# Two graph layers over one adjacency matrix: the first load of adj ahead of x, x in five parts, constants in another order

## The chip, the core and the metric

The kernel runs on one core of a Trainium2 chip. The metric is the device time of one execution in microseconds. The kernel before takes 233.75 us, the median of 3 runs (233.69 to 233.84).

## The reference

`x` has 4096 rows of 64 numbers, `adj` is 4096 x 4096 with zeros and ones (about one entry in 256 is a one), both in float32. Two layers follow one another; each adds its result to its input and normalizes every row (layernorm, no scale).

```python
# layer 0
support = x @ weight
rank = cumsum(adj != 0, axis=1); deg = rank[:, -1:]
k = minimum(deg, 100);  pos = rank - (deg - k)
w = mask * where(pos > 0, 0.5 ** (k - pos), 0)   # the last neighbour has weight 1,
x = layernorm(x + w @ support + bias)            # the one before it 1/2, then 1/4, ...
# layer 1
deg = max(sum(adj, axis=1) + 1, 1)
h = (adj @ x + x) / deg
o = relu(concat([x, h]) @ W + b);  o = o / max(norm(o), 1e-12)
x = layernorm(x + o)
```

In layer 0 the weight of a neighbour depends on how many neighbours with a higher column number the row has. So a row's sums are made from the highest column down, with a running count of the ones seen.

## The kernel before

**Tiling.** The host hands in adj transposed and cut into 8 slabs `g` of 512 rows (the output rows, along the free dimension) by 8 blocks `k` of 512 columns (the neighbours, on partitions, as 4 groups of 128). One such block is a tile `a` of 128 x 4 x 512. `load_next` (L102 to L109) fetches the next one with a DMA issued from GpSimd (POOL) that turns float32 into bfloat16: 512 KB in the core's memory, twice that in DRAM. There are 64 loads, in the order of the list `steps`: slab 0 from block 7 down to 0, then slab 1, and so on. 33 buffers hold them, three of which serve other tiles at first; 30 loads can therefore be resident. At most 8 loads are under way at a time: each load reuses the completion flag of the one eight before, so load 8 is issued when load 0 has landed. Adj stays resident because layer 1 reads each tile again.

**x.** `x` comes in two forms. `x_quads` (rows in the order in which the adj tiles hold their columns) goes to `xp`, which shares its memory with `c1`; `split_x` (L218) cuts a block of it into two float16 parts (`xhl`), with a cast, a subtraction on POOL and, in `split_x_low`, a scaling on VectorE. `x` in natural order goes to `x1` slab by slab with `load_x` (L126), and `add_b0` (L308) adds the bias of layer 0 to it. These loads and that of the weights (`load_weights`, L211) are issued from SyncE (SP), in one queue. Each DMA of `load_x` and `load_weights` first waits for a small memset of its target, which a compute engine carries out at the place in its own order where the function is called; that memset sets the time of the load.

**One step** (`g`, `k`). `count` (L317) counts the ones of a tile in 32 groups by 4 matmuls into one bank; VectorE adds the counts so far (`cs`). `spread` (L336) multiplies with `further`, a 128 x 128 matrix of zeros and ones, so that each group knows how many ones lie beyond it; ScalarE makes `near` of it. `weigh` (L343) runs 16 matmuls with `tri` (the ones within the same group) and 16 with `mine` (the group's own row of `near`) and then turns the exponent into a weight as 16-bit integers, read as bfloat16: ScalarE does two of the four groups (L367), VectorE the other two (L368). `gather` (L373) multiplies the weights of the step before with `xhl` into `acc0`. `some_sums` (L408) adds up to four matmuls of layer 1 for tiles whose `x1hl` is ready, so that the matrix engine has work while the others evict.

**Order.** Every engine's order is written out by hand. The loop over `chunks` (L711 on) runs one step after another; a chunk has one block in slabs 0 to 2, so there the count of the next step stands in each step, and up to four blocks later, so that several counts stand together. `load_next` is called once per step, ahead of the step's POOL work. `at(i, engine, fn)` hangs work into step `i` on an engine; `PLACES` overrides some of those places. Of the work named in the change: `split_x(k)` stands in steps 0 to 7 (block 7 first), `load_weights` at the end of step 1 on VectorE, `load_x(g)` in step 8g+3 and `add_b0(g)` in step 8g+7 on POOL, `prepare` (scales the weight of layer 0) in step 5, `bias_columns` in step 7, `centered_parts` (makes `wc_parts`) in step 9, `prepare_wx`, `products_parts` in step 10, `add_self(0)` in step 12, all on POOL. `early_px` (transposes with `ident16`) begins in step 3, `centered` (reads `cen`) stands in step 6, and `early_pu` (tiles `eu`, reads `wc_parts`) begins in step 9, on the matrix engine.

**Ahead of the loop.** POOL issues load 0, makes three index tables with iota (`dist`, `of_p`, `of_m`), and issues load 1 between them and loads 2 to 7 after them. SP issues x_quads in two halves of 512 KB. VectorE makes the constants one after another: `idle`, `pick`, `ident`, `cen`, `has`, `past`, `mine`, `tri`, two casts of `ident`, then `further` from the matmul `pf`. The matrix engine runs 14 matmuls on a tile of zeros, `pf`, the count of block 7, and then `warm(4)`, the spread, `warm(2)`; within step 0 `warm(4)` and `warm(3)` follow. The result of these warm-up matmuls is not used.

Of the kernel before, what the change touches and what calls it, by code (L numbers as in the profile page):

```python
# [10 lines left out]
BF16 = mybir.dt.bfloat16  # L11
# [4 lines left out]
ALU = mybir.AluOpType  # L16
# [3 lines left out]
DVE = mybir.EngineType.DVE  # L20
POOL = mybir.EngineType.Pool
SP = mybir.EngineType.SP

P = 128
R = 512
TB = R // P
KB = 4
Q = P // 4
MAX_NEIGH = 100
STEP = 128.0  # L30
# [7 lines left out]
HALVED = range(2, 7)  # L38
PLACES = {"centered_parts": (9, POOL), "prepare": (5, POOL), "bias_columns": (7, POOL), "prepare_wx": (10, POOL), "half_c1_b1 3": (38, POOL), "half_c1_b1 4": (46, POOL), "half_c1_b1 5": (57, POOL), "half_c1_b1 6": (62, POOL), "products_parts": (10, POOL), "first_mv 0": (10, "DVE, early"), "first_r 0": (11, "DVE, early"), "first_least 0": (13, "DVE, early"), "first_s 0": (11, ACT), "first_pu 0": (16, PE), "times_degree 0": (18, POOL), "first_least 1": (20, DVE), "first_pu 1": (24, PE), "first_mv 2": (28, DVE), "first_s 2": (29, ACT), "first_r 2": (29, DVE), "half_scale 2": (29, DVE), "first_x1 2": (30, POOL), "first_hi 2": (31, ACT), "first_xl 2": (31, POOL), "first_lo 2": (32, ACT), "first_least 2": (31, DVE), "half_high 2": (26, ACT), "half_rest 2": (26, DVE), "half_degree_out 2": (26, DVE), "half_degree 2": (26, PE), "half_low 2": (27, ACT), "half_pz 2": (27, PE), "half_y 2": (27, DVE), "first_x1 3": (37, POOL), "first_hi 3": (38, "ACT, late"), "first_least 3": (38, "DVE, early"), "half_low 3": (34, ACT), "half_b1 3": (38, POOL), "half_c1 3": (37, POOL), "first_s 4": (44, ACT), "half_scale 4": (45, "DVE, early"), "first_xl 4": (46, POOL), "first_least 4": (45, DVE), "first_lo 4": (47, "ACT, late"), "half_low 4": (42, ACT), "half_b1 4": (46, POOL), "first_s 5": (52, ACT), "half_scale 5": (53, DVE), "first_hi 5": (54, "ACT, late"), "first_least 5": (57, DVE), "half_low 5": (50, ACT), "half_b1 5": (52, POOL), "half_c1 5": (55, POOL), "first_s 6": (60, ACT), "first_xl 6": (62, POOL), "first_lo 6": (62, "ACT, late"), "half_low 6": (58, ACT)}
LAG = 1  # L40
SAVED = (15, 17, 18, 21, 27)


@with_exitstack
def adj_resnorm_kernel(
# [23 lines left out]
    nc = tc.nc  # L69
    D = x.shape[2]  # L70
    NG, NK = adjT.shape[0], adjT.shape[1]
# [4 lines left out]
    const = ctx.enter_context(tc.tile_pool(name="const", bufs=1))  # L76
# [25 lines left out]
    def load_next(n=1):  # L102
        for _ in range(n):
            s = next(loads, None)
            if s is None:
                return
            g, k = s
            a = a16p.tile([P, KB, R], BF16, tag="a16", name=f"a16_{g}_{k}")
            nc.gpsimd.dma_start(out=a, in_=adjT[g, k])  # L109
            A[g][k] = a  # L110
# [6 lines left out]
    xp = c1  # L117
# [1 line left out]
    prep = a16p.tile([P, KB * R // 2], F32, tag="a16", name="prep")  # L119
    xTs = [a16p.tile([P, KB, R], FP16, tag="a16", name=f"xT_{j}") for j in range(2)]  # L120

    def load_xp(k0, k1):
        bs = slice(k0 * KB, k1 * KB)
        nc.sync.dma_start(out=xp[:, bs, :], in_=x_quads[:, bs, :])

    def load_x(g):  # L126
# [1 line left out]
        nc.sync.dma_start(out=x1[:, ts(g, TB), :], in_=x[:, ts(g, TB), :])  # L128


    load_xp(NK // 2, NK)
    load_next()
    load_xp(0, NK // 2)
    dist = epi.tile([P, P], I32, tag="hT", name="dist")
    nc.gpsimd.iota(dist, [[1, P]], base=0, channel_multiplier=-1)
    load_next()
# [2 lines left out]
    nc.gpsimd.iota(of_p, [[4, KB], [4 * KB, NK], [1, 4]], base=0, channel_multiplier=-1)  # L139
    of_m = epi.tile([P, P], I32, tag="z", name="of_m")  # L140
    nc.gpsimd.iota(of_m, [[1, 4], [4 * KB, NK], [4, KB]], base=0, channel_multiplier=-1)
    load_next(6)

    idle = epi.tile([P, R], BF16, tag="near", name="idle")
    nc.vector.memset(idle, 0.0)
# [2 lines left out]
    quarters = [slice(e * Q, (e + 1) * Q) for e in range(4)]  # L148
# [10 lines left out]
    ident = epi.tile([P, P], F32, tag="near", name="ident")  # L159
    nc.vector.tensor_scalar(ident, dist, 0.0, None, ALU.is_equal)  # L160
    cen, wcf, b0T = prep[0:D, 0:D], prep[0:D, D : 2 * D], prep[0:D, 2 * D : 4 * D]
    w32, wc32 = prep[:, 4 * D : 6 * D], prep[:, 6 * D : 7 * D]
    nc.vector.tensor_scalar(cen, ident[0:D, 0:D], -1.0 / D, None, ALU.add)


    has = epi.tile([P, P], BF16, tag="y", name="has")
    nc.vector.tensor_scalar(has, of_p, 0.0, None, ALU.is_equal)
    past = epi.tile([P, P], BF16, tag="hT", name="past")
# [9 lines left out]
        else:  # L178
            nc.vector.tensor_scalar(mine[quarters[e]], one_hot, STEP, None, ALU.mult)

    tri = const.tile([P, Q], BF16, name="tri")
    for rows in quarters:
        nc.vector.tensor_scalar(tri[rows], dist[rows, rows], 0.0, -STEP, ALU.is_lt, ALU.mult)
        nc.vector.scalar_tensor_tensor(
            tri[rows], ident[rows, rows], STEP * MAX_NEIGH, tri[rows], ALU.mult, ALU.add
        )
    most = const.tile([P, 1], F32, name="most")
    nc.vector.memset(most, MAX_NEIGH)
    less = const.tile([P, 1], F32, name="less")
# [14 lines left out]
    nc.vector.memset(power, -0.5)  # L204
    x1T = const.tile([P, R], FP16, name="x1T")
    ident16 = const.tile([P, P], FP16, name="ident16")
    nc.vector.tensor_copy(ident16, ident)
    ident_b = const.tile([P, P], BF16, name="ident_b")
    nc.vector.tensor_copy(ident_b, ident)

    def load_weights():  # L211

# [104 lines left out]
    def count(g, k, first, last):  # L317
        if first:
            cnt[g] = ps_m.tile([P, R], F32, tag="m", name=f"cnt_{g}_{k}")
        for q in range(KB):  # L320
            nc.tensor.matmul(  # L321
                cnt[g][quarters[q], :],
                lhsT=pick[:, PW - 4 * k : PW - 4 * k + Q],
                rhs=A[g][k][:, q, :],
                start=first,
                stop=last,
            )
        if last:
            new = one.tile([P, R], BF16, tag="cs", name=f"cs_{g}_{k}")
            if g in cs:  # L330
                nc.vector.tensor_tensor(new, cnt[g], cs[g], ALU.add)  # L331
            else:
                nc.vector.tensor_copy(new, cnt[g])  # L333
            cs[g] = new

    def spread(g, k):  # L336

        pr = ps_m.tile([P, R], F32, tag="m", name=f"rep_{g}_{k}")
        nc.tensor.matmul(pr, lhsT=further, rhs=cs[g], start=True, stop=True)  # L339
        near[g] = epi.tile([P, R], BF16, tag="near", name=f"near_{g}_{k}")  # L340
        nc.scalar.activation(near[g], pr, AF.Relu, bias=most, scale=-1.0)  # L341
# [54 lines left out]
    def ready(i, g, b):  # L396
        k = b // KB
        return i >= low_at[k] + LAG and i >= when[g, k]

# [208 lines left out]
    def at(i, engine, fn, *args):  # L608
        i, engine = PLACES.get(" ".join([fn.__name__, *map(str, args)]), (i, engine))
        hooks[i, engine].append((fn, args))  # L610

    def run(i, engine):
        for fn, args in hooks.pop((i, engine), []):
            fn(*args)
# [5 lines left out]
    for k in range(NK):  # L620
        i = when[0, k]
        at(i, POOL, split_x, k)
        at(i, DVE, split_x_low, k)
    at(1, DVE, load_weights)
    at(NK - 2, POOL, prepare)
    at(NK + 1, POOL, prepare_wx)
    at(NK + 2, POOL, prepare_wn)
    for g in range(NG):
        at(NK * g + 3, POOL, load_x, g)
        at(NK * g + 7, POOL, add_b0, g)  # L630
        at(min(NK * g + 12, NS - 2), POOL, add_self, g)
    if HALVED:
        all_at(
# [12 lines left out]
    for g in range(NG - 1):  # L646
        i = NK * (g + 1)
# [42 lines left out]


    pi = ps_a.tile([P, R], F32, tag="acc1", name="pi")
    for i in range(14):
        nc.tensor.matmul(pi, lhsT=idle[:, 0:P], rhs=idle, start=True, stop=True)

    def warm(n):

        a = A[0][NK - 1][:, 0, :]
        for i in range(n):
            nc.tensor.matmul(pi, lhsT=a[:, 0:P], rhs=a, start=True, stop=True)  # L700
# [3 lines left out]
    further = const.tile([P, P], BF16, name="further")  # L704
    nc.vector.tensor_copy(further, pf)
    count(0, NK - 1, True, True)
    warm(4)
    spread(0, NK - 1)
    warm(2)
    held = None  # L710
    for c, chunk in enumerate(chunks):  # L711
        ahead = chunks[c + 1] if c + 1 < len(chunks) else []

        shares = [[]] * (len(chunk) - 1) + [ahead]
        nr = near[chunk[0][0]]
        for (g, k), share in zip(chunk, shares):
            i = when[g, k]
            run(i, ACT)
            load_next()
            run(i, POOL)  # L720

            w = weigh(g, k, nr) if i == 0 else None
            for s in share:
                count(*s, s == ahead[0], s == ahead[-1])
            run(i, "DVE, early")
            w = w or weigh(g, k, nr)
            run(i, "ACT, late")
            if i == 0:
                warm(4)
            n_todo = len(todo)  # L730
            done = some_sums(i, 0 if i in SAVED else QUOTA)
            half = 0
            if share and share[-1] == ahead[-1]:
                if held is not None and len(todo) == n_todo:

                    half = KB // 2
                    gather(*held, 0, half)
                spread(*ahead[-1])
            if i == 0:
                warm(3)  # L740
            if done is not None:
                evict_part(done)
            if held is not None:
                gather(*held, half)
            held = (g, k, w)
            if g > 0 and k == NK - 1:
                first_hT(g - 1)
            run(i, PE)
            run(i, DVE)
# [318 lines left out]
```

## Time and profile before

| | us |
|---|---|
| median of 3 runs | 233.75 |
| the profiled execution | 233.72 |
| its span, first to last instruction | 231.7 |
| PE busy (matmuls) | 209.5 |
| DVE busy (VectorE) | 182.2 |
| ACT busy (ScalarE) | 140.6 |
| POOL busy (GpSimd) | 112.3 |
| adj loads: 64 x 512 KB, median from issue to landing | 15.2 |
| x_quads: 2 x 512 KB, the same | 4.5 |
| x in natural order: 8 x 128 KB | 7.2 |
| weights: 192.5 KB | 7.2 |

The durations in the prediction come from the profiled execution, which is 0.03 us below the median. The page cuts the span into 40 slices of 5.8 us and gives each engine's busy share in tenths. A group names the line, the engine, the operation, output<-inputs, shapes and count, then the busy time and the mean of one in ns, then the idle time of the engine just before these instructions with what ended most of it. In a stretch's line the numbers are: its length, busy time (and number of instructions) of PE, PEld (weight loads of the matrix engine), DVE, ACT and POOL, the granted clock of the matrix engine, the busy share of the 16 DMA engines, and GB/s. The share may come out a little over 1. In the lines on queues, q0 carries the loads issued from POOL, q1 those from SP; the numbers are packets, MB, and the time of the packets as a share of 16 engines. The bytes are those written.

### The profile page before, as it was taken

The page shows a single profiled execution, that of the slowest core. Times are in us where ns is not written, and L with a number is a line of the kernel's source. Part 1 is how long each engine was busy: PE and PEld are TensorE (multiplying, and loading weights), DVE is VectorE, ACT ScalarE, POOL GpSimd, SP SyncE. Part 2 cuts the span into 40 slices and gives each one's busy share as a digit, 9 for nine tenths or more (in the row PEclk, how much of TensorE's full clock was granted, in tenths as well). Part 3 has the DMA queues.
Part 4 walks back from the last instruction along what each step waited for, and adds up shares of the span by engine and source line. Part 5 has one row for each costly group of instructions (what it writes and reads, how often), then busy time and mean ns, then how long its engine had stood idle before and what let it go on. Part 6 is the DMA issues. An engine that isn't in the chain of part 4 may idle for free.

```text
span 231.7 us, 7494 instructions
## 1 busy us (share of the span) xinstructions
PE 209.5 (90%) x3138; PEld 95.2 (41%) x3178; DVE 182.2 (79%) x454; ACT 140.6 (61%) x212; POOL 112.3 (48%) x211
## 2 busy tenths in 40 slices
PE   7589999998998999999999999999999999999910
PEld 2133445443533443334333433443334344776810
DVE  6459877997797789798975996687678866599983
ACT  6057886687778767686557455664675451142684
POOL 7439677761537081641584056325433040079970
PEclk9799999999999999999999999999999999999975
DMA  6999999999999999999999999999970000000013
GB/s 201 209 213 219 215 216 213 217 217 214 215 219 212 214 214 223 211 214 214 218 217 207 200 183 210 204 195 181 205 168 4 3 0 0 3 0 1 23 45 113
DMA packets 11984, 37.36 MB, mean 161 GB/s; under 512 B 1328, under 2 KB 3504, under 8 KB 11952
## 3 DMA queue, kind: packets, MB, share of 16 engines
q0 software_dynamic: 9216, 33.56, 73.7%
q1 hardware_dynamic: 2736, 3.34, 4.7%
q8 instruction: 24, 0.39, 0.6%
q14 instruction: 8, 0.07, 0.1%
HBM read 69.40 MB, written 1.05 MB: 304 GB/s over the span
## 4 chain that ended last, share of the span: by engine, by line
PE 40%; DVE 11%; POOL 4%; ACT 3%; issue 2%; ACTq 0%; DVEq 0%; POOLq 0%
PE acc L378 12%; PE acc_part L387 11%; PE v L351 5%; PE cnt L321 3%; PE v L360 3%; ACT u L961 2%; POOL scratch L947 2%; DVE w L368 2%; POOL scratch L978 2%; DVE cs L331 1%; PE rep L339 1%; PE va L930 1%; PE pz L505 1%; PE vb L387 1%; DVE part L403 1%
## 5 line engine op out<-in xcount | busy, mean ns | idle before, releaser
L367 ACT ACTIVATE w<-v,less 128x1024 int16<-128x1024 f32 x64 | 71.3, 1113 | 43.7 <-PE v L360 31.7
L368 DVE TENSOR_SCALAR w<-v 128x1024 int16<-128x1024 f32 x64 | 78.2, 1221 | 13.0 <-PE v L360 12.1
L378 PE MATMUL acc<-w,xhl 128*128 128x512 bf16 x235 | 65.2, 380 | 1.9 <-issue 1.1
L109 POOL DMA_DIRECT2D a<-in_adjT_dram x64 | 36.9, 622 | 48.2 <-PE acc_part L387 25.4
L387 PE MATMUL acc_part<-a,x1hl 128*128 128x512 bf16 x140 | 38.2, 381 | 1.8 <-issue 1.3
L378 PEld LDWEIGHTS <-xhl 128*128 128x128 f16 x256 | 23.1, 98 | 33.6 <-issue 9.7
L341 ACT ACTIVATE near<-rep,most 128x512 bf16<-128x512 f32 x40 | 27.3, 682 | 8.7 <-PE rep L339 8.6
L387 PEld LDWEIGHTS <-x1hl 128*128 128x128 f16 x224 | 18.6, 98 | 31.1 <-issue 13.3
L351 PE MATMUL v<-a,tri 32*32 32x512 bf16 x1024 | 29.6, 384 | 0.3 <-DVE w L368 0.2
L360 PE MATMUL v<-near,mine 32*32 32x512 bf16 x1024 | 28.1, 376 | 0.0
L331 DVE TENSOR_TENSOR cs<-cnt,cs 128x512 bf16<-128x512 f32 x32 | 21.9, 686 | 4.4 <-PE cnt L321 4.0
L321 PE MATMUL cnt<-a,pick 128*32 128x512 bf16 x256 | 21.4, 389 | 4.2 <-DMA a<-in_adjT_dram 2.9
L351 PEld LDWEIGHTS <-tri 32*32 32x32 bf16 x1024 | 9.5, 87 | 21.7 <-issue 21.5
L339 PE MATMUL rep<-cs,further 128*128 128x512 bf16 x40 | 15.4, 385 | 1.5 <-DVE cs L331 1.1
L565 POOL TENSOR_SCALAR x<-y,mv_l,r_l 128x64 f32<-128x64 f32 x16 | 9.1, 575 | 12.4 <-DVE dr L516 6.4
L947 POOL TENSOR_TENSOR scratch<-scratch,power 128x4 f32<-128x4 f32 (+1 forms) x5 | 6.4, 1279 | 15.2 <-DVE scratch L949 15.1
L306 POOL TENSOR_TENSOR a<-a,ident_b 128x128 bf16<-128x128 bf16 x32 | 12.7, 431 | 0.1
L321 PEld LDWEIGHTS <-pick 128*32 128x32 bf16 x256 | 5.9, 94 | 14.8 <-issue 11.3
L333 DVE CAST cs<-cnt 128x512 bf16<-128x512 f32 x8 | 5.5, 692 | 7.8 <-PE cnt L321 7.8
L360 PEld LDWEIGHTS <-mine 32*32 32x32 bf16 x1024 | 10.2, 87 | 2.8 <-issue 2.4
L961 ACT ACTIVATE u<-u,scratch 128x64 f32<-128x64 f32 x27 | 9.8, 428 | 2.2 <-POOL scratch L980 2.1
L944 ACT ACTIVATE u<-u 128x256 f32<-128x256 f32 (+1 forms) x5 | 2.5, 502 | 12.1 <-DVE u L933 12.1
(177 smaller groups left out, 272.2 us busy)
## 6 DMA issues: line engine op xcount, KB each, us to landing
a<-in_adjT_dram POOLq DMA_DIRECT2D x64, 512.0 KB, 15.2
c<-in_x_quads_dram SPq DMA_DIRECT2D x2, 512.0 KB, 4.5
x<-in_x_dram SPq DMA_DIRECT2D x8, 128.0 KB, 7.2
out_dram<-u SPq DMA_DIRECT2D x8, 128.0 KB, 1.7
wts<-in_weights_dram SPq DMA_DIRECT2D x1, 192.5 KB, 7.2
```

Source lines behind the costliest of these rows:

```text
L109: nc.gpsimd.dma_start(out=a, in_=adjT[g, k])
L321: nc.tensor.matmul(cnt[g][quarters[q], :], lhsT=pick[:, PW - 4 * k : PW - 4 * k + Q], rhs=A[g][k][:, q, :], start=first, stop=last,)
L331: nc.vector.tensor_tensor(new, cnt[g], cs[g], ALU.add)
L339: nc.tensor.matmul(pr, lhsT=further, rhs=cs[g], start=True, stop=True)
L341: nc.scalar.activation(near[g], pr, AF.Relu, bias=most, scale=-1.0)
L351: nc.tensor.matmul(v[e // 2][quarters[q], e % 2, :], lhsT=tri[quarters[e], :], rhs=A[g][k][quarters[e], q, :], start=True, stop=False,)
L360: nc.tensor.matmul(v[e // 2][quarters[q], e % 2, :], lhsT=mine[quarters[e], 4 * k + q, :], rhs=nr[quarters[e], :], start=False, stop=True,)
L367: nc.scalar.activation(w[:, 0:2, :], v[0], AF.Relu, bias=less)
L368: nc.vector.tensor_scalar(w[:, 2:4, :], v[1], -STEP * MAX_NEIGH, 0.0, ALU.add, ALU.max)
L378: nc.tensor.matmul(acc0[g], lhsT=xhl[:, b, :], rhs=w[:, q, :].bitcast(BF16), start=(k, q) == (NK - 1, 0), stop=(k, q) == (0, KB - 1),)
L387: nc.tensor.matmul(acc, lhsT=x1hl[:, b, :], rhs=A[g][b // KB][:, b % KB, :], start=first, stop=last)
L961: nc.scalar.activation(o[:, t, :], y[:, t, :], AF.Identity, bias=off[:, t : t + 1], scale=r[:, t : t + 1])
```

## The change

- The first load of adj stands ahead of x in the program. The first SP load is the piece of x_quads for block 7 alone (128 KB). The other pieces (block 6; blocks 5 and 4; 3 and 2; 1 and 0) each wait for a memset on POOL: three of these stand between loads 2 to 7, the last in step 1.
- On VectorE `tri` is made right after `ident`, ahead of `has` and `past`; `cen` and the two casts of `ident` move behind the count of block 7, just ahead of the loop.
- The idle matmuls become 8 (were 14), and the later warm-up groups 1, 2, 3 and 3 (were 4, 2, 4 and 3).
- The weights are asked for in step 2 (was 1), the natural x of slab 0 in step 5 (was 3), and its bias is added in step 8 (was 7).

The parts of the program that compute are otherwise as before.

```diff
+WARM = 8, 1, 2, 3, 3
...
-    def load_xp(k0, k1):
+    def load_xp(k0, k1, held=True):
         bs = slice(k0 * KB, k1 * KB)
+        if held:
+            nc.gpsimd.memset(xp[:, k0 * KB, 0:1], 0.0)
         nc.sync.dma_start(out=xp[:, bs, :], in_=x_quads[:, bs, :])
...
-    load_xp(NK // 2, NK)
     load_next()
-    load_xp(0, NK // 2)
+    load_xp(NK - 1, NK, False)
     dist = epi.tile([P, P], I32, tag="hT", name="dist")
...
-    load_next(6)
+    load_next(2)
+    load_xp(NK - 2, NK - 1)
+    load_next(2)
+    load_xp(NK - 4, NK - 2)
+    load_next(2)
+    load_xp(NK - 6, NK - 4)
...
-    nc.vector.tensor_scalar(cen, ident[0:D, 0:D], -1.0 / D, None, ALU.add)
-
-
+
+    tri = const.tile([P, Q], BF16, name="tri")
+    for rows in quarters:
+        nc.vector.tensor_scalar(tri[rows], dist[rows, rows], 0.0, -STEP, ALU.is_lt, ALU.mult)
+        nc.vector.scalar_tensor_tensor(
+            tri[rows], ident[rows, rows], STEP * MAX_NEIGH, tri[rows], ALU.mult, ALU.add
+        )
     has = epi.tile([P, P], BF16, tag="y", name="has")
...
-    tri = const.tile([P, Q], BF16, name="tri")
-    for rows in quarters:
...
-    nc.vector.tensor_copy(ident16, ident)
...
-    nc.vector.tensor_copy(ident_b, ident)
...
-    at(1, DVE, load_weights)
+    at(1, POOL, load_xp, 0, NK - 6)
+    at(2, DVE, load_weights)
...
-        at(NK * g + 3, POOL, load_x, g)
-        at(NK * g + 7, POOL, add_b0, g)
+        at(NK * g + 3 if g else 5, POOL, load_x, g)
+        at(NK * g + 7 if g else 8, POOL, add_b0, g)
...
-    for i in range(14):
+    for i in range(WARM[0]):
...
-    warm(4)
+    warm(WARM[1])
     spread(0, NK - 1)
-    warm(2)
+    warm(WARM[2])
+    nc.vector.tensor_scalar(cen, ident[0:D, 0:D], -1.0 / D, None, ALU.add)
+    nc.vector.tensor_copy(ident16, ident)
+    nc.vector.tensor_copy(ident_b, ident)
     held = None
...
             if i == 0:
-                warm(4)
+                warm(WARM[3])
...
             if i == 0:
-                warm(3)
+                warm(WARM[4])
```

More of the change, by code (lines that the diff above doesn't have):

```diff
@@ L179, in adj_resnorm_kernel @@
             nc.vector.tensor_scalar(mine[quarters[e]], one_hot, STEP, None, ALU.mult)
-    tri = const.tile([P, Q], BF16, name="tri")
-    for rows in quarters:
[L183 to L186, printed above, removed]
     most = const.tile([P, 1], F32, name="most")
```

## The prediction

> **What bounds the kernel now.** I read the page first: its slices for where the time lies, its groups for who waits.
>
> ```profile
> PE   7589999998998999999999999999999999999910
> DMA  6999999999999999999999999999970000000013
> L321 PE MATMUL cnt<-a,pick 128*32 128x512 bf16 x256 | 21.4, 389 | 4.2 <-DMA a<-in_adjT_dram 2.9
> a<-in_adjT_dram POOLq DMA_DIRECT2D x64, 512.0 KB, 15.2
> ```
>
> Two rows are nearly full at once, the matmuls and the DMA engines, so it has to be settled which of them paces which stretch. Second view, stretches of time (length, busy time of PE, PEld, DVE, ACT, POOL, clock, DMA share, GB/s):
>
> ```profile
> 0.00:2.50 2.50, 1.32 (x4) 0.49 (x5) 0.71 (x10) 1.49 (x2) 1.35 (x7) 1.00 0.22 64
> 12.00:20.00 8.00, 6.98 (x125) 2.57 (x126) 5.38 (x9) 5.24 (x8) 4.53 (x8) 1.00 1.07 215
> 36.00:60.00 24.00, 22.69 (x429) 10.84 (x432) 20.30 (x41) 17.29 (x26) 14.14 (x31) 1.00 1.06 216
> 90.00:112.00 22.00, 21.12 (x356) 8.16 (x360) 19.57 (x43) 15.09 (x20) 7.68 (x14) 1.00 1.06 213
> 112.00:120.00 8.00, 7.80 (x125) 2.86 (x140) 6.40 (x14) 4.31 (x7) 6.66 (x13) 1.00 1.07 220
> 172.00:190.00 18.00, 17.79 (x275) 7.41 (x278) 15.83 (x37) 9.65 (x14) 4.80 (x9) 1.00 0.03 8
> ```
>
> The DMA share is above 1 from 2.5 us to beyond 120: one unbroken stream, in which a load of adj (0.524 MB) lands every 2.45 us. Third view, the order of time around the first count of each new load (start, length, engine, line, [idle before and what ended it]), and how long the loads issued at 9.2 and at 109.8 take to land:
>
> ```profile
> 8.94 0.62 PE L321 MATMUL cnt<-a,pick 128*32 128x512 bf16 x4 [2.67 <-DMA a<-in_adjT_dram]
> 27.87 0.10 PEld L321 LDWEIGHTS <-pick 128*32 128x32 bf16 x4 [0.45 <-DMA a<-in_adjT_dram]
> 30.62 0.23 PEld L321 LDWEIGHTS <-pick 128*32 128x32 bf16 x4 [0.17 <-DMA a<-in_adjT_dram]
> 118.80 1.05 PE L321 MATMUL cnt<-a,pick 128*32 128x512 bf16 x16
> ```
> ```profile
> L109 POOL DMA_DIRECT2D a<-in_adjT_dram x1: 535/535/535, 9.2 to 9.2; - x1
> ...
> DMA to landing us min/median/max: 21.4/21.4/21.4
> ...
> L109 POOL DMA_DIRECT2D a<-in_adjT_dram x1: 530/530/530, 109.8 to 109.8; - x1
> ...
> DMA to landing us min/median/max: 9.6/9.6/9.6
> ```
>
> TensorE waits 2.67 us for the first load (it lands at 1.23 + 7.7 = 8.9). It then catches up with the stream and waits for loads 7 and 8 (counted from 0; load 8 lands at 9.2 + 21.4 = 30.6, its count starts at 30.75). Load 10 lands at 17.2 + 18.4 = 35.6 and its count starts at 35.88. From there TensorE is slower than the stream and falls some us behind (the load issued at 53.46 lands 19.8 later at 73.2 and is counted at 77.3), until at 118.80 it wants loads 40 to 43 in a row: load 43 lands at 109.8 + 9.6 = 119.4, in the middle of those 1.05 us. So the stream touches the work at 28 to 36 us and again at 119; only a change that brings the stream forward brings the end forward.
>
> **The change part by part.** The 8 early adj loads and x share the 16 DMA engines, so I keep a ledger of the stream, in us of all 16 engines.
>
> Before, where adj starts: queue q0 (adj) had moved this much in the first 6 us and in the next 6, q1 (SP) beside it:
>
> ```profile
> q1 hardware_dynamic: 287, 1.05, 55.8%
> q0 software_dynamic: 35, 0.14, 13.0%
> ...
> q0 software_dynamic: 343, 1.27, 106.7%
> ```
>
> 1.41 MB by 12.0 us is 6.6 us at 214 GB/s: adj runs as if it had started at 5.4 at full rate. The 1.05 MB of x took 55.8% of 6 us, 3.35 us, before it.
>
> After, start S: one 128 KB piece of x goes first (first packets 1.7 us, about 0.5 us long) and adj load 0 is issued at 1.23 as before. What an adj load takes to its first packet on empty engines no row shows. Lower end: SP's x, issued at 0.73, has first packets at 1.7, so 1.0 us, S = 2.2. Upper end: as now, with no adj packet before 4.8, S = 4.9. Between: on busy engines the weights, issued at 18.57, have no packet before 21.4, about 2 us more than the 1.0 on empty ones, so I take the 2 off 4.9: S = 2.9.
>
> The Trainium skill ("DMA: Bandwidth & Descriptors", Latency and other measured facts) gives about 1 us to the first byte on this path; by it S would be 2.2 and the sum below -0.5 us. The row of 18.57 is weighed higher, as it is this kernel's.
>
> Cost X of the other 0.92 MB of x, now inside the stream: at the best pace of x alone (0.59 MB in 1.5 us, 404 GB/s) 2.3 us; at the price of the later x loads (128 KB in 1 KB packets; four of them 2.0% of 96 us, so 0.48 each) seven times 0.48, 3.4 us. One piece is such a 1 KB one, three have 2 KB packets, priced in between at 0.75: X = 0.48 + 2.25 = 2.7.
>
> Shift of the stream: (2.9 - 5.4) + 2.7 = +0.2 us. Ends: (2.2 - 5.4) + 2.3 = -0.9 and (4.9 - 5.4) + 3.4 = +2.9, the last only if x leaves the engines empty for 2.5 us.
>
> A rule that speaks against the change is in the same page (Rules for kernel authors): many small transfers should be one large one, at 2.0 us fixed per DMA. Three more DMAs would by it be +6 us and 239.9. The x rows above show 0.48 us of engine time for a whole one beside adj, so that figure is not used.
>
> What is gained on the way and lost again: load 0 lands at 2.9 + 2.45 + 1.1 = 6.5, 2.4 us earlier. The warm-up after the first count goes from 4 matmuls to 1; four of them ran 9.49 to 11.17 while the spread's input was ready at 10.29, so 0.9 us more. Step 1 starts some 3 us earlier. Steps 1 to 6 take 2.3 us each (counts at 16.0, 18.1, 20.4, 22.9, 25.2), so TensorE would be at count 6 by 22.5, and load 6 lands at about 25.2. All of the lead is waited away there.
>
> Work in cover of that lead: 8 instead of 14 idle matmuls (0.43 each): TensorE only waits for load 0 afterwards. The clock reads 0.67 and 0.65 in 7.5 to 12.5 now; a second stretch at half speed would double about 1.7 us of matmuls in step 1, and the 3 us pay for it. Constants: cen (1.25) and the two casts (0.23, 0.22) leave the way of `further` (ends 7.81, then about 6.5, load 0's own time) for DVE's 2.85 us of idleness before 13.14; without that cover they would cost 1.7. Four memsets of 0.1 on POOL and the later issue of loads 2 to 7: two loads, 5 us of transfer, are ahead of each. Where x comes late: the piece for step 1 is issued near 5 and by the later x rows (7.2 to landing) is there at 12, ScalarE's cast of it due at 16.08 - 3 = 13; behind that cast stand the evictions of step 1. The next pieces follow on SP's queue about 3.3 us apart (weights and x of slab 0, issued at 18.6 and 20.8, landed at 25.7 and 29.4) and are up to 1 us late for steps 2 and 4; the lead pays.
>
> SP's queue is now four pieces, weights, x of slab 0. The weights are asked for one step later in steps that come 2 to 3 us sooner: landing unchanged at 25.7, POOL's wait for them (1.64) too. x of slab 0 is two steps later, behind that wait: 25.7 + 0.95 (two multiplies) + 0.1, so issue near 26.8 instead of 20.8, landing 7.1 to 8.6 later at 33.9 to 35.4. Its 0.48 us leaves the stream ahead of load 8 and is back by load 10. add_b0, in step 8 now, waits for it on POOL (it had no wait at 30.21), and behind it stand load 17 (33.33 now; 7 loads still under way), centered_parts (1.53) and all to 40.2. 34.8 to 36.3 + 0.57 + 1.53 = 36.9 to 38.4 for wc_parts, which TensorE reads at 38.21: free, barely. POOL's backlog ends in its 1.48 us of idleness before 44.48.
>
> Sum: stream +0.2 us at loads 10 to 43, less nothing to speak of (0.06) at 119. Profiled execution: 233.72 (span 231.7 and 2.0 around it), the median 233.75. 233.75 + 0.2 = 233.95, said as 234.0. A shift under 0.2% (0.47 us) is about what a measurement of this kernel can tell from none.
>
> **The rivals.**
> - The stream gets longer (slower). For: adj's first packets may need more than 1.7 us, small packets are dear. Against: the first half of x was itself slow to start. It decides from S = 3.2 at X = 2.7; middle S = 3.6, X = 3.0: +1.2, 234.9.
> - x of slab 0 holds POOL, and wc_parts holds TensorE at 38.2 (slower). It decides when x lands after 35.2; if the weights land 1.5 us later than now, 1.7 us are lost, 235.4. For: the one queue in order. Against: the pieces ahead should be through by 21.4.
> - The stream gets shorter (faster): S = 2.2 to 2.5 and X = 2.3 to 2.5, -0.4 to -0.9, 232.85 to 233.35. For: the idle engines in 0 to 1.7 us and the 1.0 us of SP. Against: x takes 2.3 us wherever it stands.
> - All of the 2.4 us at load 0 stays (231.4). Against: the two waits at 27.87 and 30.62 and the tie at 119.4.
>
> **How the numbers follow.** No change to speak of 40% (233.3 to 234.2); longer stream 27% and POOL held 11%, slower together 38%; shorter stream 20% and full gain 2%, faster 22%. Leaving out 10% at either end, the range is 232.9 to 235.2: the low end is the -0.9, the high end +1.4, between the two slower rivals.
>
> **What would show it.** The first count at 6.5 (right start) with counts 7 and 8 still waiting for DMA at 27.9 and 30.7 within 0.5 us: right. Load 43 landing near 119.6 and the count of 40 to 43 tied to it: right. First load after 7.5, or load 10 after 36.3: longer stream. add_b0 idle to after 35 and `eu` idle on POOL: the second rival. Counts at 28 to 36 over 0.5 us earlier without waits: I have the stream wrong. It would also be wrong if the order of the middle steps shifts against each other in a way that no row here foretells.

## The result and the profile after

The kernel after takes 234.90 us (median of 7 runs, 234.60 to 236.17); the kernel before, on the same chip, 233.69 us (233.49 to 233.84). The ratio is 1.0059, 95% interval 1.0040 to 1.0079: slower by 1.2 us, about 0.5%. The profiled execution took 235.29 us with a span of 232.8; the span grew by 1.1 us. The time lies in the predicted range, but the case that I held likeliest (no change to speak of, 233.95) did not come; the first rival (the stream gets longer, 234.9) did, to the tenth. The tenth is chance: that rival had the start S at 3.6 and the price X at 3.0, and the runs give 3.0 and 3.6 (below).

The page after: the slices of the matrix engine and of the DMA engines, the group of the counts, the loads of adj.

```profile
PE   6776999998998999999999999999999999999920
DMA  5999999999999999999999999999990000000013
L324 PE MATMUL cnt<-a,pick 128*32 128x512 bf16 x256 | 21.6, 392 | 4.4 <-DMA a<-in_adjT_dram 3.2
a<-in_adjT_dram POOLq DMA_DIRECT2D x64, 512.0 KB, 15.7
```

L324 is the former L321. The wait of the counts for adj is nearly the same in sum (3.2 us, 2.9 before), but it stands elsewhere. The stretches show it (columns as before: length, PE, PEld, DVE, ACT, POOL, clock, DMA share, GB/s):

```profile
8.00:12.00 4.00, 3.19 (x41) 0.87 (x42) 1.98 (x6) 2.09 (x3) 1.20 (x2) 1.00 1.05 183
12.00:20.00 8.00, 5.12 (x85) 1.70 (x85) 4.82 (x9) 4.36 (x6) 4.01 (x8) 1.00 1.04 241
20.00:24.00 4.00, 3.46 (x42) 1.00 (x43) 2.12 (x3) 1.46 (x2) 1.91 (x4) 0.57 1.06 242
90.00:112.00 22.00, 21.17 (x374) 8.43 (x392) 19.23 (x39) 15.06 (x21) 7.66 (x14) 1.00 1.07 215
112.00:120.00 8.00, 7.81 (x128) 2.70 (x97) 7.03 (x20) 4.60 (x6) 5.36 (x11) 1.00 1.06 217
```

From 12 to 20 us the matrix engine is busy for 5.12 us, before 6.98. From 90 us on all is as it was. The order of time around the counts (start, length, engine, line, [idle before, releaser]), and the loads issued at 6.6, 7.3 and 111.1:

```profile
6.59 0.62 PE L324 MATMUL cnt<-a,pick 128*32 128x512 bf16 x4 [0.40 <-DMA a<-in_adjT_dram]
16.14 0.40 PE L324 MATMUL cnt<-a,pick 128*32 128x512 bf16 x4 [0.56 <-DMA a<-in_adjT_dram]
20.54 0.62 PE L324 MATMUL cnt<-a,pick 128*32 128x512 bf16 x4 [2.23 <-DMA a<-in_adjT_dram]
120.11 1.05 PE L324 MATMUL cnt<-a,pick 128*32 128x512 bf16 x16
```
```profile
L110 POOL DMA_DIRECT2D a<-in_adjT_dram x2: 535/621/707, 6.6 to 7.3; - x2
...
DMA to landing us min/median/max: 22.3/23.2/24.1
...
L110 POOL DMA_DIRECT2D a<-in_adjT_dram x1: 527/527/527, 111.1 to 111.1; - x1
...
DMA to landing us min/median/max: 9.6/9.6/9.6
```

Against the kernel before, in us:

| load | landing before | after | shift of landing | shift of its count |
|---|---|---|---|---|
| 0 | 8.90 | 6.55 | -2.35 | -2.35 |
| 2 | 13.88 | 12.96 | -0.92 | -2.55 |
| 4 | 18.76 | 20.49 | +1.73 | +0.19 |
| 7 | 27.83 | 28.94 | +1.11 | +1.11 |
| 8 | 30.58 | 31.45 | +0.87 | +1.11 |
| 10 | 35.55 | 36.74 | +1.19 | +1.11 |
| 43 | 119.39 | 120.72 | +1.33 | +1.32 |

The lead of the first load is there and is gone by load 4, which the matrix engine awaits for 2.23 us. From 20.35 us on the granted clock is at half for 3.4 us (0.57 in the row of 20 to 24; before, one such stretch stood at 8.4 to 11.8). It costs nothing in the end, but only just: the counts of loads 6 and 7 come 0.09 and 0.04 us after the landings, with no idle time ahead of them. From load 9 on the stream is about 1.2 us behind, and the work keeps that to load 43 and the end. The memsets on POOL do not hold the loads up: loads 2 to 7 are issued from 3.64 to 6.61 us, before from 3.65 to 6.61.

Where do 1.2 us of stream go? The two DMA queues (q0 adj, q1 from SP; packets, MB, share of the 16 engines) in 0 to 8 and in 8 to 24 us, before and then after:

```profile
q1 hardware_dynamic: 288, 1.05, 41.9%
q0 software_dynamic: 148, 0.57, 37.1%
...
q0 software_dynamic: 904, 3.28, 102.2%
q1 hardware_dynamic: 97, 0.15, 2.9%
```
```profile
q0 software_dynamic: 254, 0.97, 66.5%
q1 hardware_dynamic: 144, 0.13, 5.6%
...
q0 software_dynamic: 713, 2.59, 84.2%
q1 hardware_dynamic: 643, 1.02, 20.5%
```

A ledger in us of all 16 engines: q1 took 3.35 + 0.46 = 3.81 before and 0.45 + 3.28 = 3.73 after, for 1.20 and 1.15 MB. Byte for byte x costs the engines the same, ahead of adj or among it. But adj has moved 3.85 MB by 24 us before and 3.56 after, 0.29 MB less, which is 1.45 us at its rate. Two things make that up. The first: in the first 8 us the engines are busy for 5.77 us instead of 6.32 (and for 22.52 instead of 23.13 by 24 us): x, which comes on fast, used a time in which adj alone does not fill the engines. With what x took less, that is 0.53 us. Most of it lies between 2.4 and 3.6 us (before, then after; the last two numbers are the share of the DMA engines and GB/s):

```profile
2.40:3.60 1.20, 1.20 (x4) 0.44 (x3) 1.15 (x3) 0.93 (x1) 1.18 (x3) 1.00 0.97 242
2.40:3.60 1.20, 1.20 (x4) 0.45 (x3) 1.19 (x2) 0.93 (x1) 1.19 (x3) 1.00 0.68 78
```

The second: a MB of adj took 5.28 us of engine time instead of 5.02, on 3.56 MB 0.92 us: adj's own packets were slower for a while, some 0.4 us of it at the start of the stream (the first took 0.6 to 1.2 us each, later ones 0.32) and nearly 0.6 us from 9 to 13 us. A part (0.2 to 0.3 us) is given back between 24 and 32 us, where before's packets are slower beside x of slab 0.

### The profile page after: what moved, and what is told of

It reads as the page before. It is cut to its first block, busy times and chain, and to the rows that moved or that the text cites. A ratio compares the mean times of both kernels' runs of the same rounds, so it can differ in the third digit from the quotient of the medians.

```text
span 232.8 us, 7486 instructions
## 1 busy us (share of the span) xinstructions
PE 208.6 (90%) x3128; PEld 94.1 (40%) x3168; DVE 182.6 (78%) x454; ACT 140.8 (60%) x212; POOL 111.8 (48%) x215
## 4 chain that ended last, share of the span: by engine, by line
PE 40%; DVE 10%; POOL 4%; ACT 3%; issue 2%; ACTq 0%; DVEq 0%; POOLq 0%
PE acc L381 12%; PE acc_part L390 11%; PE v L354 5%; PE cnt L324 3%; PE v L363 3%; ACT u L968 2%; POOL scratch L954 2%; DVE w L371 2%; POOL scratch L985 2%; DVE cs L334 1%; PE rep L342 1%; PE va L937 1%; PE pz L508 1%; PE vb L390 1%; DVE part L406 1%
## 5 line engine op out<-in xcount | busy, mean ns | idle before, releaser
L354 PE MATMUL v<-a,tri 32*32 32x512 bf16 x1024 | 30.1, 391 | 0.5 <-DVE w L371 0.5
L324 PE MATMUL cnt<-a,pick 128*32 128x512 bf16 x256 | 21.6, 392 | 4.4 <-DMA a<-in_adjT_dram 3.2
L568 POOL TENSOR_SCALAR x<-y,mv_l,r_l 128x64 f32<-128x64 f32 x16 | 9.0, 572 | 11.8 <-DVE dr L519 6.4
L309 POOL TENSOR_TENSOR a<-a,ident_b 128x128 bf16<-128x128 bf16 x32 | 12.6, 430 | 0.1
L324 PEld LDWEIGHTS <-pick 128*32 128x32 bf16 x256 | 5.9, 94 | 15.4 <-issue 8.0
```

Source lines behind the costliest of these rows:

```text
L324: nc.tensor.matmul(cnt[g][quarters[q], :], lhsT=pick[:, PW - 4 * k : PW - 4 * k + Q], rhs=A[g][k][:, q, :], start=first, stop=last,)
L354: nc.tensor.matmul(v[e // 2][quarters[q], e % 2, :], lhsT=tri[quarters[e], :], rhs=A[g][k][quarters[e], q, :], start=True, stop=False,)
```

## The experiments

My theory after the result (theory A in the first expectations): the parts of x inside the stream lengthen it. Its rivals are these: the weights and natural x asked for later hold POOL and the matrix engine (theory B there); the constants and the warm-ups; and, inside theory A, whether the number of packets or something else is the price. "Before" below is the kernel before, timed beside each group of runs (233.84, 233.90 and 233.78 us). Each run has one profiled execution, and it is not always a typical one; where it was not, the text says so.

**The x part alone.** The kernel before with the first load ahead and x in five parts; constants, warm-ups, weights and x of slab 0 as before.

```diff
-    load_xp(NK // 2, NK)
     load_next()
-    load_xp(0, NK // 2)
+    load_xp(NK - 1, NK, False)
...
-    load_next(6)
+    load_next(2)
+    load_xp(NK - 2, NK - 1)
+    load_next(2)
+    load_xp(NK - 4, NK - 2)
+    load_next(2)
+    load_xp(NK - 6, NK - 4)
...
+    at(1, POOL, load_xp, 0, NK - 6)
```

> The kernel before with the change to x alone (adj first, five pieces, four of them held by memsets); all else as before. Theory A (the x pieces in the stream): 234.9 (234.5 to 235.2), first count near 6.6 to 7.0, load 8 landing some 0.9 later than before at 31.4. Theory B (the other parts): 233.7.

234.93 us (5 runs, 234.72 to 235.12), ratio 1.0048 [1.0036, 1.0060]. The landings of adj are 1.4 us late, the counts 1.67 us from load 7 on. This part by itself gives the whole loss. Its trace also speaks against the clock as the cause: with the same five parts the clock was full from 6.2 us on, and the counts of loads 3 to 7 all start 0.04 us after their landings.

**All but the x part.** The kernel after with x in two halves at the head of the stream.

```diff
+    load_xp(NK // 2, NK, False)
     load_next()
-    load_xp(NK - 1, NK, False)
+    load_xp(0, NK // 2, False)
...
+    load_next(6)
...
-    at(1, POOL, load_xp, 0, NK - 6)
```

> The changed kernel with x put back as it was (two halves of 512 KB ahead of the adj loads, no memsets for them); constants, warm-up matmuls, weights and natural x stay as changed. Theory A, the place and the pieces of x in the DMA stream set the time: 233.7 (233.4 to 234.0), first load lands at 8.9 again, counts 7 and 8 wait for DMA at 27.9 and 30.7. Theory B, the other parts (constants, fewer warm-up matmuls, later weights and natural x) set it: it stays at 234.9.

237.53 us (5 runs), ratio 1.0154 [1.0136, 1.0173]: neither theory had foreseen it. The landings of adj are as before or, from load 5 to load 42, mostly 0.1 to 0.9 us earlier. The order of time (the profiled execution, 238.03 us, is the longest of the five):

```profile
29.42 0.39 POOL L228 TENSOR_SCALAR wts<-wts 64x64 f32<-64x64 f32 x1 [5.26 <-DMA wts<-in_weights_dram]
...
33.06 0.61 PE L377 MATMUL acc<-w,xhl 128*128 128x512 bf16 x2 [1.60 <-DVE xhl L225]
...
39.04 0.72 POOL L310 TENSOR_TENSOR x<-x,wts 128x256 f32<-128x256 f32 x1 [4.20 <-DMA x<-in_x_dram]
...
41.49 0.19 PE L294 MATMUL eu<-wc_parts,xT 128*128 128x64 f16 x1 [1.56 <-POOL wc_parts L254]
```

POOL waits 5.26 us for the weights, and behind it stands the splitting of x that the gather on the matrix engine reads; then POOL waits 4.20 us for x of slab 0, and `wc_parts` holds the matrix engine. That is my second rival, in full. In the kernel after it does not occur because its first steps come 2 to 3 us earlier, and with them the requests: the weights are asked for at 18.81 us there, at 21.24 here (18.57 before). The later places of these requests fit only the earlier start.

**The constants and the warm-ups alone.** As the run just told, but the weights, x of slab 0 and its bias at their places of before.

```diff
+    load_xp(NK // 2, NK, False)
     load_next()
-    load_xp(NK - 1, NK, False)
+    load_xp(0, NK // 2, False)
...
-    at(2, DVE, load_weights)
+    at(1, DVE, load_weights)
...
-        at(NK * g + 3 if g else 5, POOL, load_x, g)
-        at(NK * g + 7 if g else 8, POOL, add_b0, g)
+        at(NK * g + 3, POOL, load_x, g)
+        at(NK * g + 7, POOL, add_b0, g)
```

> The kernel before with the other order of the constants and the shorter warm-ups of the changed kernel alone: x in two halves at the head of the stream, the weights at step 1, x of slab 0 at step 3, add_b0 at step 7. Stream theory: load 0 lands at 8.9 us and the rest of the stream as before, so 233.7 us (233.4 to 234.0). If the constants' order or the warm-ups cost anything (a clock that falls at another place, the tri constant ahead of others), it shows here: 234.1 or more.

233.73 us (12 runs), ratio 0.9999 [0.9983, 1.0016]: nothing. Its trace shows the second place where the stream is touched. Up to count 42 the matrix engine is 0.18 us ahead of the kernel before, and then:

```profile
118.60 0.83 PE L320 MATMUL cnt<-a,pick 128*32 128x512 bf16 x12
119.76 0.40 PE L320 MATMUL cnt<-a,pick 128*32 128x512 bf16 x4 [0.33 <-DMA a<-in_adjT_dram]
```

The sixteen matmuls that stood in one row at 118.80 before are torn in two: load 43 lands 0.33 us later than before (a wobble of the stream), and the rest of the run is 0.31 us late. In this run a gain on the matrix engine alone did not pass 119 us.

**The weights and natural x earlier again.** The kernel after, only these requests moved back.

```diff
-    at(2, DVE, load_weights)
+    at(1, DVE, load_weights)
...
-        at(NK * g + 3 if g else 5, POOL, load_x, g)
-        at(NK * g + 7 if g else 8, POOL, add_b0, g)
+        at(NK * g + 3, POOL, load_x, g)
+        at(NK * g + 7, POOL, add_b0, g)
```

> The changed kernel with x in its five parts, but the weights asked for at step 1, x of slab 0 at step 3 and add_b0 at step 7, as in the kernel before. If the five parts of x inside the stream of adj are what costs (stream theory): the landings of loads 8 to 43 stay 1.2 to 1.7 us later than before, count 43 too, and the time is 234.7 to 235.0 us; the 0.22 us that the late add_self adds at step 13 may go, without effect at the end, since load 43 sets it. If the weights and x asked for later are what costs: back to 233.7.

235.25 us (8 runs), ratio 1.0051 [1.0033, 1.0069], a little above what was expected of the stream theory. Nothing comes back: the 128 KB of natural x now pass ahead of load 7, which lands at 29.94 instead of 28.94, and the counts are 2.1 us late from there to load 50. That is from the longest of the eight executions (236.73 us); the median is only 1.35 us late. The additional shift of 0.2 us at count 14 (below) is gone here, as expected.

```profile
29.98 0.40 PE L324 MATMUL cnt<-a,pick 128*32 128x512 bf16 x4 [0.99 <-DMA a<-in_adjT_dram]
```

**Fewer and larger parts of x.** The kernel after with the seven other blocks in two parts, of four and three blocks.

```diff
-    load_xp(NK - 2, NK - 1)
+    load_xp(NK - 5, NK - 1)
...
-    load_xp(NK - 4, NK - 2)
...
-    load_xp(NK - 6, NK - 4)
+    load_xp(0, NK - 5)
...
-    at(1, POOL, load_xp, 0, NK - 6)
```

> The changed kernel with the x behind the first piece in two pieces (blocks 6 to 3 with rows of 4 KB behind loads 2 and 3; blocks 2 to 0 with rows of 3 KB behind load 7) instead of four. Same bytes, 256 packets instead of 512. If a packet of x costs by itself: 0.8 us less of the engines, so 234.1 (233.8 to 234.4). If x costs by its bytes: 234.9, no difference from the changed kernel. Theory B: 234.9 too.

234.52 us (9 runs), ratio 1.0037 [1.0023, 1.0052]: by the median better than after, though the two intervals overlap, and not the 234.1 expected. The stream itself is only 0.5 to 0.7 us late at loads 9 to 13, about as expected by packets: in 8 to 24 us q1 takes 16.9% (0.99 MB), 2.70 us instead of 3.28. But load 7 still lands at 28.89, 1.06 us late, and the matrix engine keeps that. Why load 7 is that late is not shown: load 8, behind the same parts of x and the weights, is late by 0.15 us only.

**No other x at all.** Two runs leave blocks 6 to 0 of x out of layer 0 (zeros stand for them). In the first, the zeros are written by the memsets on POOL.

```diff
         if held:
-            nc.gpsimd.memset(xp[:, k0 * KB, 0:1], 0.0)
-        nc.sync.dma_start(out=xp[:, bs, :], in_=x_quads[:, bs, :])
+            nc.gpsimd.memset(xp[:, bs, :], 0.0)
+        else:
+            nc.sync.dma_start(out=xp[:, bs, :], in_=x_quads[:, bs, :])
```

> The changed kernel without the transfers of x behind the first piece: a memset of the whole piece stands in place of the DMA, so the blocks 6 to 0 of x count as zeros in layer 0. Theory A: the early start is kept, the stream lies 2.4 us ahead of before and TensorE with it, 231.4 (231.0 to 232.0), no more than 0.5 us of waiting for loads 7 and 8. Theory B: 234.9, as nothing of the rest is changed. If the stream is not what bounds after 36 us: 232.5 to 233.7.

238.28 us (4 runs), ratio 1.0192 [1.0163, 1.0220], and inconclusive on the time: the long memsets kept the constants back (the first count at 8.64 us although load 0 had landed at 6.58), the steps did not come early, and the late requests for the weights and x cost what they cost in the run with x at the head. Its stream can be read: the landings are 2.1 to 3.1 us earlier than before for loads 0 to 12 and 1.7 to 2.3 for loads 13 to 19.

In the second, ScalarE writes the zeros after the constants, and weights, natural x and bias stand where they did before.

```diff
-        if held:
-            nc.gpsimd.memset(xp[:, k0 * KB, 0:1], 0.0)
-        nc.sync.dma_start(out=xp[:, bs, :], in_=x_quads[:, bs, :])
+        if not held:
+            nc.sync.dma_start(out=xp[:, bs, :], in_=x_quads[:, bs, :])
...
+    rest = slice(0, (NK - 1) * KB)
+    nc.scalar.mul(xp[:, rest, :], zero.unsqueeze(2).to_broadcast([P, (NK - 1) * KB, D]), 0.0)
...
+    at(1, DVE, load_weights)
...
+        at(NK * g + 3, POOL, load_x, g)
+        at(NK * g + 7, POOL, add_b0, g)
```

> The changed kernel without any of the parts of x behind the first (blocks 6 to 0 of x count as zeros in layer 0, written on chip by ScalarE: that part of the computation is left out), with the weights, x of slab 0 and add_b0 at their places of before. Stream theory: the landings of adj come 2.0 to 2.4 us earlier than before at all loads, TensorE follows them, and the time is 231.4 us (231.0 to 232.0), so that the parts of x are worth 3.3 to 3.5 us. If TensorE could not use an earlier stream because something else sets it after the start (constants, clock, weights), it stays above 232.7.

232.24 us (4 runs, 232.15 to 232.28), ratio 0.9926 [0.9906, 0.9945]. The matrix engine does follow an earlier stream, to the end, and waits for it at the old places:

```profile
26.18 0.40 PE L325 MATMUL cnt<-a,pick 128*32 128x512 bf16 x4 [0.92 <-DMA a<-in_adjT_dram]
29.21 0.40 PE L325 MATMUL cnt<-a,pick 128*32 128x512 bf16 x4 [0.28 <-DMA a<-in_adjT_dram]
```

The stream is 1.45 us earlier than before at loads 8 to 43, not the 2.0 to 2.4 expected: load 0 landed at 6.99 here, 0.4 us later than in the other runs that begin with it, and between loads 6 and 8, which the weights and natural x share, the lead of the stream fell from 2.16 to 1.41 us. Between this run and the kernel after, the four other parts of x are worth 2.7 us of stream (1.27 + 1.45); the first of the two runs makes it about 3.3. The clean run began later and lost time of its own, so its 2.7 is a lower figure (more on this below).

**Half of x ahead, half held.** An attempt at a better mixture: before, with one edit.

```diff
     load_xp(NK // 2, NK)
     load_next()
-    load_xp(0, NK // 2)
...
-    load_next(6)
+    load_next(2)
+    load_xp(0, NK // 2, True)
+    load_next(4)
```

> The kernel before with one edit: the first half of x stays ahead of load 0, the second half is asked for only behind loads 1 and 2 in the program, held by a one-column memset on POOL that makes its DMA wait for the two index patterns there. Stream theory: load 0 starts about 1.2 to 1.4 us earlier (5.4 to about 4.1), the second half, in rows of 4 KB, costs the stream 1.0 to 1.5 us later instead of ahead of it, so the loads from 8 on shift by -0.3 to +0.3: 233.5 us (233.2 to 234.0). If any x inside the stream costs it more than x ahead of it, whatever the rows: 234.2 or more.

234.39 us (12 runs), ratio 1.0016 [0.9996, 1.0036]; by the profile the counts are 0.58 us late from load 6 on, the landings 0.25 to 0.3 us at loads 8 to 12. Load 0 landed at 8.93, as before: its first packets started 1.2 us earlier (3.79 instead of 4.98) but took 1.4 to 1.9 us each, instead of the later 0.32. In the first 8 us this kernel moves 148 GB/s, before 203. The median lies where the expectation has an x ahead of adj cheaper than the same x inside, even in rows of 4 KB; since the interval takes in no change at all, that is not shown.

**The slow packets of adj.** In the kernel after a packet of adj (4 KB as written) took 0.40 to 0.47 us from 9.5 to 12 us, beside the second part of x, and 0.32 otherwise. The queues from 10 to 12 us after:

```profile
q0 software_dynamic: 68, 0.25, 85.6%
q1 hardware_dynamic: 71, 0.07, 18.0%
```

0.25 MB took 85.6% of 2 us, 6.8 us a MB. The same stretch in the second run without the other x (the same stream, no x beside it), and in the run with half of x held (x beside it in rows of 4 KB):

```profile
q0 software_dynamic: 120, 0.43, 106.3%
```
```profile
q0 software_dynamic: 72, 0.26, 64.6%
q1 hardware_dynamic: 74, 0.30, 39.5%
```

4.9 and 5.0 us a MB: neither is slow. To see whether the slow packets belong to that part of x or to that time, the parts were asked for two loads later.

```diff
-    load_next(2)
+    load_next(4)
     load_xp(NK - 2, NK - 1)
     load_next(2)
     load_xp(NK - 4, NK - 2)
-    load_next(2)
     load_xp(NK - 6, NK - 4)
```

> The changed kernel with its second and third part of x asked for two loads later in the program (behind six and eight loads instead of four and six), nothing else. In the changed kernel the packets of adj took 0.40 to 0.47 us instead of 0.32 from 9.5 to 12 us, beside the second part of x, which cost the stream 0.6 us. If that belongs to this part of x: it moves with it to about 11 to 14 us and the stream stays about 1.2 us late at loads 8 to 13, 234.7 to 235.1 us (more if steps 1 and 2 wait for x longer than the lead of TensorE covers). If it belongs to what else runs from 9.5 to 12 us: the slow packets stay at that time and are fewer, or go, and the stream is 0.4 to 0.6 us earlier, 234.3 to 234.6.

235.01 us (8 runs), ratio 1.0047 [1.0028, 1.0067]. The slow packets moved with the part of x, to 11 to 13.5 us; here they are in 11 to 13 us:

```profile
q0 software_dynamic: 70, 0.23, 64.7%
q1 hardware_dynamic: 75, 0.08, 16.7%
```

5.6 us a MB, slower than 4.9 but less so than in the kernel after; summed, adj's packets took 0.24 us more than 0.32 each between 10 and 14 us, in the kernel after 0.54. (This profile is of the shortest of the eight executions, 234.29 us, so the size may not be typical.) The time is the same within the intervals, as the first reading has it. So in these two profiles the slowing goes with the part of x, and its size varies. What makes it is open: the run with x in two parts has it too (0.36 to 0.43 us a packet, rows of 4 KB), the parts with rows of 2 KB that follow in the kernel after do not.

**Natural x of slab 4 behind load 43.** On top of the constants alone.

```diff
-        at(NK * g + 3, POOL, load_x, g)
-        at(NK * g + 7, POOL, add_b0, g)
+        at(38 if g == 4 else NK * g + 3, POOL, load_x, g)
+        at(41 if g == 4 else NK * g + 7, POOL, add_b0, g)
```

> The constants-only kernel (x in halves at the head, constants and warm-ups of the changed kernel) with one more edit: x of slab 4 is asked for at step 38 instead of 35 and its add_b0 runs at step 41 instead of 39, so that its 128 KB pass behind load 43. In the constants-only run TensorE was 0.18 us ahead of the kernel before up to count 42, and load 43 then took that away and 0.3 more. If the tie at load 43 is a real second gate of the stream: load 43 lands 0.3 to 0.5 us earlier than there, TensorE keeps its lead, count 43 at -0.2 against the kernel before, and the time is 233.5 us (233.3 to 233.6). If the end is set by something else: no change, 233.7.

233.41 us (12 runs, 233.24 to 234.22), ratio 0.9985 [0.9972, 0.9999]: the fastest of the kernels that compute all of it, by 0.4 us against before, with an interval that just leaves 1 out. It is not clear of the run that it is built on (the constants alone, 0.9983 to 1.0016). That the tie at load 43 is what gives way is not shown: the profiled execution is one of the longer ones (its load 0 landed 0.31 us late), and in it load 42 came 0.12 us earlier than before and load 43 0.24 us later.

## Why the prediction was right and wrong

**Right: which resource sets the end.** The stream touches the work at 28 to 36 us and at 119, and only its shift counts. Counts 7 and 43 shifted with their landings (+1.11 and +1.11; +1.32 and +1.33), and the clean run without the other x followed its stream by -1.45. The place at 28 us is narrower than I had it: it is load 7 alone. Count 8 follows count 7 by 2.87 us before and after alike, so load 8, whose landing shifted by only 0.87, holds nothing; in the clean run, with 3.03 us between the two counts, it does. The lead (2.6 us at count 1, 3 predicted) was waited away, 2.23 us of it ahead of load 4, two loads sooner than I had it.

**Right in size, by luck in its make-up: the start S.** Load 0 landed at 6.55 us, predicted 6.5 with S = 2.9. But the 2 us taken off 4.9 are not what the trace shows: the first packet of adj starts at 2.71 us, 1.5 us after its issue and just behind x's first piece (last packet 2.67), and the first eight packets took 0.6 to 1.2 us each. By the figure of the Trainium skill for the first byte, about 1 us ("DMA: Bandwidth & Descriptors", Latency and other measured facts), the estimate would have been 5.8. With x's piece on the engines ahead of adj, no run here shows that figure by itself.

**Too low: X, the price of x inside the stream, 2.7 us.** From load 1, which no later part of x can delay yet (-2.41), to loads 9 to 12 (+1.2 to +1.3) the stream lost 3.6 to 3.7 us. The packets of x themselves took 2.9 us of engine time, 0.59 for the part in rows of 1 KB and 2.30 for the three with 2 KB: the prices of 0.48 and 0.75 were nearly right. Some 0.6 us more is that adj's own packets became slower beside the second part of x; 0.1 to 0.2 I can't assign. So (2.9 - 5.4) + 2.7 = +0.2 became (3.0 - 5.4) + 3.6 = +1.2.

The sum had no term for adj's packets becoming slower, and the kernel before could have shown one. From 25 to 28 us, beside natural x of slab 0, its queues are:

```profile
q0 software_dynamic: 132, 0.48, 88.9%
q1 hardware_dynamic: 131, 0.13, 16.7%
```

That is 5.6 us a MB of adj instead of 5.0. How much of the 3.6 us is the price of x depends on what it is held against. The clean run without the other x makes it 2.7, the number predicted. That run's load 1 was at -1.90 instead of -2.41, and from there to load 9 (-1.46) it lost 0.44 us without any of these parts; from 24 to 26 us, beside natural x, its adj packets cost 6.7 us a MB.

**The ledger says it shorter.** x costs the engines the same wherever it stands (3.81 against 3.73 us with the part of the weights), so a later x could win only time in which the engines stand idle. That time grew, by 0.5 us, because adj comes on slowly (a share of 0.68 against 0.97 from 2.4 to 3.6 us). This much was in the prediction (2.9 us of x leave the front, the start moves by only 2.5); that adj itself becomes dearer was not.

**The rule against the change.** The rule of the Trainium skill for kernel authors ("DMA: Bandwidth & Descriptors", Rules for kernel authors), one large transfer instead of many small, had given an estimate of +6 us, at the 2.0 us of fixed cost a DMA that the same page has under Anatomy of one DMA. Three more DMAs cost 1.2 us in all, and the run with x in three DMAs, one more than before, 0.7. Its direction agrees, its size does not: beside the stream a part of 128 KB took 0.59 us of engine time.

**Right, and for its reason: POOL and `wc_parts`.** The prediction had x of slab 0 issued near 26.8 and landing at 33.9 to 35.4, and `wc_parts` "free, barely". The order of time after (POOL, PE and DVE):

```profile
35.13 0.72 POOL L314 TENSOR_TENSOR x<-x,wts 128x256 f32<-128x256 f32 x1 [2.82 <-DMA x<-in_x_dram]
37.62 0.30 POOL L259 TENSOR_TENSOR wc_parts<-prep,wc_parts 128x64 f16<-128x64 f32 x1
39.31 0.40 PE L298 MATMUL eu<-wc_parts,xT 128*128 128x64 f16 x8
...
43.42 1.59 POOL L309 TENSOR_TENSOR a<-a,ident_b 128x128 bf16<-128x128 bf16 x4
44.65 0.39 DVE L436 TENSOR_TENSOR q_l<-s_l 128x4 f32<-128x4 f32 x1
```

It was issued at 27.8 and landed at 35.05 (the weights ahead of it at 26.7, 1.0 us later than I had said, with the stream); `wc_parts` ended at 37.9, the matrix engine read it at 39.31 without a wait. What I missed is small: the backlog puts `add_self` (L309) 2.0 us later, beside VectorE's chain for the first rows of layer 0. Before, these stood apart:

```profile
41.41 1.59 POOL L306 TENSOR_TENSOR a<-a,ident_b 128x128 bf16<-128x128 bf16 x4
43.55 0.15 DVE L433 TENSOR_TENSOR q_l<-s_l 128x4 f32<-128x4 f32 x1
```

The small product took 0.39 instead of 0.15 us, and the counts from load 14 on are 0.2 us later than those ahead (+1.33 against +1.11). The Trainium skill ("SBUF — State Buffer", SBUF: two separate sides) has a VectorE instruction with two inputs in that memory and a GpSimd instruction that reads it lock each other out for a whole instruction. This trace agrees: the product starts inside the last of the four adds, ends at 45.04 when that add ends (45.01), and takes 0.24 us longer. It does not add to the time, since load 43, at +1.33 itself, takes it in; in the run with the weights earlier, with the counts 2.1 us late, load 43 still landed at +1.29.

**Costed at nothing, and nothing.** Constants and warm-ups: 0.9999. The half clock after the long wait: it began at 20.4 us instead of 8.4, and brought the work to count 7 just as load 7 landed. The run with the x part alone had no such stretch there and took as long.

**The chances.** Longer stream had 27%, the largest of the rivals; its point of decision, S = 3.2 at X = 2.7, was passed through X and not through S.

## What to carry over

When two streams share the DMA engines, set up one ledger of engine time for the same bytes in both orders; a reordering can win only time in which the engines stand idle, and loses whatever the slower starter leaves unused. A load moved among others costs its own packets and may slow those beside it; by the medians x in fewer, larger parts lost less (0.7 against 1.2 us), with intervals that overlap. Parts of a change can lean on each other: the later requests cost 3.8 us where the earlier start was taken away, and bringing them forward in the changed kernel won nothing.

## What the runs showed of the hardware

- Packets of adj took 0.40 to 0.47 us instead of 0.32 beside one part of x, and went back to 0.32 beside the next parts, in rows of 2 KB. Moved by two loads, the slowing moved along, at half the size in the one profile there is. Beside the 128 KB of natural x of slab 0 they took 0.35 to 0.40 us in the kernel before and 0.41 to 0.48 in the clean run, but 0.32 in the kernel after. The cause is open.
- With adj behind 128 KB of x the 16 engines moved 106 to 113 GB/s in the first 5.8 us in all runs of that kind, with all of x ahead of it 200. Idle engines are only a part of that: a packet of 4 KB of x there took 0.21 us on average (most 0.16), one of adj 0.32. Once both ran they moved up to 248 (16 to 20 us after), adj alone 211 to 217.
- Small parts beside the full stream land late: in the kernel after the second part's first packet came 3.8 us after its issue, and the four later parts landed 8.1 to 13.2 us after they were issued, in the kernel before, at the head of the stream, the halves after 3.8 and 5.2.
